# A graph attention layer's sums: from the planner's order to an order fixed in the source, with shares a chunk ahead and edge sums a chunk behind

## The chip, the cores and the metric

The kernel runs on one NeuronCore of a Trainium2 chip. Five engines run their own instruction queues side by side: TensorE (PE, matrix products; PEld is its loading of weights), VectorE (DVE), ScalarE (ACT), GpSimd (POOL) and SyncE (SP, which here only starts transfers). They wait for one another by semaphores, and each takes its own queue strictly in the order in which the program was laid down. The metric is the device time of one execution in microseconds (us); the median of the runs counts.

## The reference

Two graph layers over 6250 nodes with 128 features and 100000 edges, sorted by destination. The first is a pair of graph convolutions; this case is about the second, an attention layer, cut here to what matters:

```
z = h @ fc_w.T                      # 6250 x 128
rh = r_h @ fc_r_w.T                 # 100000 x 128, r_h are the edges' own features
e = leaky_relu(z[src] @ aw[0] + z[dst] @ aw[1] + rh @ aw[2])
ex = exp(e - segment_max(e, dst)[dst])
alpha = ex / segment_sum(ex, dst)[dst]
agg = segment_sum(alpha[:, None] * (z[src] + rh), dst)
out = relu(agg + z @ loop_w)        # then x = layernorm(x + out)
```

## The kernel before

The edges are cut into 49 chunks (`NC`) of 2048. Every chunk's destinations lie in a window of 144 nodes (`WC`), so what a chunk adds goes into 144 columns of a transposed sum (`acc2` for the node part, `sum_r` for the edge part). The program has four stages, one after the other: preparing and sorting the slots of the edges, the first convolution, the second convolution, and the attention. The second convolution runs under `tc.manual_schedule()`, that is, its instructions stay in the order of the source. In all other stages a planner at compile time places the instructions of each engine by its own priorities and costs, within the data's dependencies and the number of buffers; it may pull work far ahead of its place in the source. The change lies in the last stage (L979 to L1239), from about 1426 us of the span to the end.

**The work of one chunk** in that stage:

- `shares` (L1147): the weights of the softmax are brought into the slots' order. DVE makes two one-hot masks (`ohm` L1150, `ohg` L1152) and their product with the weights (`put` L1155); PE sums over them in 16 products (L1159); DVE reduces the result to `swt` (L1160).
- `pick` (L451): the rows z[src]. For 12 of the 17 slot groups of a chunk they are picked from the table `hot` in SBUF by 144 small products with one-hot masks (L460, three parts of four groups, each in a PSUM tile `g`); ACT copies them out with their weight (`got`, L465). The other five groups are gathered from DRAM by POOL (`far`, L469). DVE makes the one-hot window mask `wm` (L474).
- `weigh` (L478) multiplies the mask of the five gathered groups by `swt` on ACT; `scatter` (L484) sums a chunk's 17 groups into its window, 34 products on PE in one PSUM tile `win`. Both are done for the chunk before (`held`).
- `edge_part` (L1162): loads the edges' features in two halves (`et`, 512 KB each, L1171), makes the masks `ms` (L1176, L1178) and `pl` (L1180) on DVE, sums the edges in 32 products (`r`, L1189), has ACT copy the result (`sw`, L1194), and places it in the window with four products (L1200).
- `add_in` (L491) adds a window into `acc2` or `sum_r` on DVE (L493).
- `Pieces` and `out_of` (L412, L429) finish the output of four blocks of 128 nodes as soon as all their edges are in: load `fin`, products (`agg`, L421), addition and layer norm, store.

**The scores** for the softmax are a second stream of work, written as a generator `scores()` that stops at each `yield`. It goes batch by batch: `batches` has 2, 5 and then 7 chunks at a time. For each batch it does `ends` for the destinations (four chunks at a time; a load `dk`, a mask L1012, products L1017, a dozen small DVE instructions, a store `adg`), `starts` for the sources (each chunk in two halves: a load `rk` of 256 KB, DVE's mask L1038 and `ohb` L1040, 24 products L1045 into the tile `k`, DVE's `sel` L1048 and reduction `asr` L1049), and `softmax` over the rows of the batch (L1053: a load `ad`, five scans on DVE with products on PE between them, an exponential on ACT, a store `shd` and a load `al` in another layout). The scores of batch b+1 are dealt out beside the chunks of batch b, in the source at four places of each chunk (`beside`, `deal`). Since this stage is not under `manual_schedule`, that placing is the planner's first order only.

Of the kernel before, what the change touches and what calls it, by code (L numbers as in the profile page):

```python
# [9 lines left out]
F32 = mybir.dt.float32  # L10
# [9 lines left out]
P = 128  # L20
# [18 lines left out]
def gnn_kernel(ctx, tc, x, src, dst, ea, ew, W1, b1, W2, b2, fcw, fcrw, attn, loopw, out):  # L39
# [372 lines left out]
    def out_of(sum_x, sum_r, b0, n, xp, pool, tag):  # L412
# [6 lines left out]
        for b, nb in some:  # L419
            of = slice(b * P, b * P + nb)  # L420
            nc.tensor.matmul(agg[:nb, b - b0, :], sum_r[:, of], wfrT, start=True, stop=False)  # L421
            nc.tensor.matmul(agg[:nb, b - b0, :], sum_x[:, of], ident, start=False, stop=True)
        for p, k in whole(some, b0):
# [5 lines left out]
    class Pieces:  # L429
# [3 lines left out]
        def __init__(self, start):  # L433
            self.ahead = [(min((b0 + n) * P, N), start(b0, n)) for b0, n in groups]
            self.at = None
            next(self.ahead[0][1])

        def go(self, low, steps):

            while steps > 0:  # L440
                if self.at is None:
# [3 lines left out]
                    if self.ahead:  # L445
# [5 lines left out]
    def pick(c, mask, hot, table, ps_g, wp, gots=4, fars=12):  # L451

        rows = []
        for g0 in range(0, GP, 4):
# [11 lines left out]
            rows += [got[:, g, :] for g in range(n)]  # L466
        for g in range(GS):
# [5 lines left out]
        wm = wp.tile([P, G, WC], F32, name="wm")  # L473
        nc.vector.tensor_tensor(wm, iota[:, None, :WC].to_broadcast([P, G, WC]),  # L474
                                sdst[:, c, :, None].to_broadcast([P, G, WC]), op=OP.is_equal)
# [8 lines left out]
    def scatter(held, ps_w):  # L484
# [4 lines left out]
        return ps  # L489
# [490 lines left out]
    with tc.tile_pool(name="look", bufs=2) as lp, tc.tile_pool(name="conv3", bufs=2) as wp, \  # L980
            tc.tile_pool(name="mov", bufs=2) as mp, tc.tile_pool(name="outp", bufs=2) as xp, \
            tc.tile_pool(name="ps_g3", bufs=3, space=PSUM) as ps_g, tc.tile_pool(name="ps_w3", bufs=1, space=PSUM) as ps_w, \
            tc.tile_pool(name="ps_r3", bufs=1, space=PSUM) as ps_r, tc.tile_pool(name="ps_k3", bufs=1, space=PSUM) as ps_k, \
            tc.tile_pool(name="ps_c3", bufs=2, space=PSUM) as ps_c:
# [22 lines left out]
        def ends(c0, n):  # L1007
# [5 lines left out]
            ps = ps_c.tile([P, 4, J, NK], F32, name="rec")  # L1013
# [18 lines left out]
        def starts(c):  # L1032

            for h in range(2):
# [6 lines left out]
                                        op=OP.is_equal)  # L1041
                ps = ps_k.tile([P, NL // 2, NB], F32, name="k")
# [10 lines left out]
        def softmax(b):  # L1053
# [5 lines left out]
            ps = ps_c.tile([P, P], F32, name="rec")  # L1059
# [12 lines left out]
            def moved(k, of, way):  # L1072

                ps = ps_c.tile([P, 1], F32, name="rec")
# [6 lines left out]
            def spread(of, k):  # L1081

                nc.vector.tensor_tensor(of, of, end, op=OP.mult)
                nc.vector.tensor_tensor_scan(full[:, ::-1], go[:, ::-1], of[:, ::-1], 0.0, op0=OP.mult, op1=OP.add)
                ps = moved(k, full[:, 0:1], behind)
# [6 lines left out]
            nc.vector.tensor_tensor_scan(part, bias, e, -BIG, op0=OP.add, op1=OP.max)  # L1092
            ps = moved(0, part[:, P - 1 :], before)
# [8 lines left out]
            nc.vector.tensor_tensor_scan(part, first, e, 0.0, op0=OP.mult, op1=OP.add)  # L1102
# [306 lines left out]
```

## Time and profile before

| | us |
|---|---|
| median of 14 runs | 2312.17 (2294.31 to 2326.83) |
| the profiled execution | 2302.72 |
| its span | 2300.8 |
| granted clock of TensorE, mean | 0.865 |

How to read the lines below: in a timeline each line is a start, a duration, an engine, a line of the kernel, an operation, what it writes and reads, its shape, and how many in a row; in brackets stands how long the engine was idle before it, and what ended that. In a table of stretches each line has the stretch and its length, then for each engine the busy time and in brackets the count of instructions, then the granted clock of TensorE as a share, the share in which the DMA engines were busy and the GB/s that they moved. In a table of groups the busy time and the mean duration of one (in ns) follow the bar, then the idle time of the engine just before them and who ended it.

### The profile page before, as it was taken

What the parts mean: (1) busy time and instruction counts of PE and PEld (TensorE: products, weight loads), DVE (VectorE), ACT (ScalarE), POOL (GpSimd) and SP (SyncE); (2) the same over time, 40 slices, a digit from 0 to 9 for tenths busy, and PEclk for the clock granted to TensorE, in tenths of its full rate; (3) what the DMA queues carried; (4) which work ended last, traced back from release to release, by engine and by line L of the source; (5) the groups of instructions that cost most, each with busy time, mean ns of one, the idle gap of its engine ahead of it and who ended that gap; (6) DMA issues with size and microseconds to landing.
All of it is one profiled execution on the core that took longest, in us unless ns stands there. A gap on an engine that the chain in (4) does not pass through costs nothing.

```text
span 2300.8 us, 78659 instructions
## 1 busy us (share of the span) xinstructions
PE 1776.5 (77%) x33861; PEld 1546.2 (67%) x33861; DVE 1695.5 (74%) x3105; ACT 993.5 (43%) x3096; POOL 1185.3 (52%) x929
## 2 busy tenths in 40 slices
PE   3677788887988786788888883368887888888886
PEld 2465677776877665677777772367777777777775
DVE  8749786785867327788988874688787788787663
ACT  1106445444554554466666662023333333334443
POOL 4003655767766627768878760214243344436662
PEclk9758799998998877889999995579899898889998
DMA  3001433333343316576666765645555556555552
GB/s 82 2 1 57 131 88 114 86 94 91 82 122 111 110 54 216 154 210 225 223 205 219 227 187 94 148 128 159 152 148 148 141 145 167 143 148 144 153 158 66
DMA packets 260706, 306.79 MB, mean 133 GB/s; under 512 B 44121, under 2 KB 199372, under 8 KB 253299
## 3 DMA queue, kind: packets, MB, share of 16 engines
q1 hardware_dynamic: 228741, 244.80, 35.2%
q0 software_dynamic: 23520, 48.22, 10.2%
q10 hardware_dynamic: 8088, 8.65, 1.2%
q8 instruction: 268, 4.39, 0.8%
q14 instruction: 89, 0.73, 0.1%
HBM read 260.35 MB, written 41.23 MB: 131 GB/s over the span
## 4 chain that ended last, share of the span: by engine, by line
PE 44%; DVE 12%; issue 8%; DMA 6%; ACT 3%; another core or an unknown queue 2%; DVEq 0%; SPq 0%; POOL 0%; ACTq 0%
PE win L488 18%; PE g L460 13%; DVE wm L474 2%; PE rec L1159 2%; PE k L1045 2%; DVE sel L1048 2%; PE r L1189 2%; DMA et<-in_edge_attr_dram 2%; PE rec L1200 2%; PE mm L317 1%; DMA hz<-part 1%; ACT got L465 1%; DMA dk<-drow 1%; DVE asr L1049 1%
## 5 line engine op out<-in xcount | busy, mean ns | idle before, releaser
L469 POOL DMA_INDIRECT far<-g,sidx x490 | 766.2, 1564 | 312.2 <-PE win L488 183.2
L465 ACT ACTIVATE got<-g,swt 128x128 f32<-128x128 f32 x1764 | 489.6, 380 | 560.8 <-PE g L460 242.9
L460 PE MATMUL g<-hot,mask 128*32 128x128 bf16 x21168 | 503.3, 235 | 218.0 <-issue 200.9
L469 POOL DMA_INDIRECT far<-zd,sidx x245 | 345.7, 1411 | 531.4 <-PE win L488 402.9
L460 PEld LDWEIGHTS <-mask 128*32 128x32 bf16 x21168 | 379.2, 103 | 320.2 <-issue 300.3
L488 PE MATMUL win<-wm,got 128*128 128x144 f32 x3528 | 528.7, 308 | 5.5 <-issue 3.9
L488 PEld LDWEIGHTS win<-wm,got 128*128 128x128 f32 x3528 | 493.3, 207 | 26.3 <-issue 17.4
L474 DVE TENSOR_TENSOR wm<-iota,sdst 128x2448 f32<-128x2448 f32 x147 | 396.9, 2700 | 4.4 <-DMA g<-rows 4.4
L482 ACT ACTIVATE wm<-wm,swt 128x144 f32<-128x144 f32 x735 | 255.7, 427 | 76.4 <-DVE swt L1160 47.6
L488 PE MATMUL win<-wm,far 128*128 128x144 f32 x1470 | 208.0, 287 | 8.4 <-DMA far<-g,sidx 7.2
L488 PEld LDWEIGHTS win<-wm,far 128*128 128x128 f32 x1470 | 191.2, 190 | 10.2 <-issue 8.8
L1045 PE MATMUL k<-adp,rk 128*128 128x49 bf16 x2352 | 102.5, 198 | 79.2 <-DVE sel L1048 55.8
L1045 PEld LDWEIGHTS <-rk 128*128 128x128 bf16 x2352 | 90.5, 105 | 96.0 <-issue 53.1
L493 DVE TENSOR_TENSOR acc<-acc,win 128x144 f32 x147 | 44.1, 300 | 145.7 <-PE win L488 132.8
L306 POOL TENSOR_TENSOR hot<-low,hot 128x512 bf16<-128x512 f32 x24 | 42.2, 1758 | 200.0 <-DVE own L681 129.2
L931 DVE TENSOR_TENSOR et<-et,ar_row 128x2048 f32<-128x2048 f32 (+1 forms) x49 | 111.6, 2278 | 23.1 <-DMA et<-in_edge_attr_dram 21.5
L932 DVE TENSOR_REDUCE dots<-et 128x16 f32<-128x2048 f32 (+1 forms) x49 | 112.0, 2286 | 1.7
L1048 DVE TENSOR_TENSOR sel<-k,ohb 128x392 f32<-128x392 f32 x98 | 83.6, 853 | 29.3 <-PE k L1045 17.5
L730 PE MATMUL rec<-put,ohm 128*128 128x90 bf16 x784 | 62.1, 253 | 28.2 <-DVE put L726 26.6
L730 PEld LDWEIGHTS <-ohm 128*128 128x128 bf16 x784 | 57.1, 165 | 34.7 <-DVE put L726 29.0
L723 DVE TENSOR_TENSOR put<-ohg,rec 128x1360 bf16<-128x1360 bf16 x49 | 76.8, 1567 | 0.0
L676 ACT CAST own<-r 128x768 bf16<-128x768 f32 x49 | 39.6, 808 | 82.5 <-PE r L673 42.9
(380 smaller groups left out, 2312.8 us busy)
## 6 DMA issues: line engine op xcount, KB each, us to landing
et<-in_edge_attr_dram SPq DMA_DIRECT2D x97, 512.0 KB
et<-in_edge_attr_dram SPq DMA_DIRECT2D x48, 1024.0 KB
mask<-masks SPq DMA_DIRECT2D x98, 384.0 KB
rk<-srow SPq DMA_DIRECT2D x98, 256.0 KB
mask<-srd SPq DMA_DIRECT2D x49, 384.0 KB
masks<-mask SPq DMA_DIRECT2D x49, 384.0 KB
far<-g,sidx POOLq DMA_INDIRECT x490
g<-rows SPq DMA_DIRECT2D x24, 256.0 KB
```

The lines of the kernel that those rows point to most:

```text
L460: nc.tensor.matmul(ps[32 * q : 32 * q + 32, g, :], mask[:, (g0 + g) * P + 32 * q : (g0 + g) * P + 32 * q + 32], hot[:, 4 * (g0 + g) + q, k ...
L465: nc.scalar.activation(got[:, g, :], ps[:, g, :], AF.Copy, scale=swt[:, c, g0 + g : g0 + g + 1])
L469: nc.gpsimd.indirect_dma_start(out=got, out_offset=None, in_=table[:, :], in_offset=bass.IndirectOffsetOnAxis(ap=sidx[:, c, g : g + 1], ax ...
L474: nc.vector.tensor_tensor(wm, iota[:, None, :WC].to_broadcast([P, G, WC]), sdst[:, c, :, None].to_broadcast([P, G, WC]), op=OP.is_equal)
L482: nc.scalar.activation(wm[:, g, :], wm[:, g, :], AF.Copy, scale=swt[:, c, g : g + 1])
L488: nc.tensor.matmul(ps, rows[g], wm[:, g, :], start=g == 0, stop=g == G - 1)
L723: nc.vector.tensor_tensor(put[:, :, : G * F].rearrange("p t (g f) -> p t g f", f=F), ohg[:, :, :, None].to_broadcast([P, TC, G, F]), rec[: ...
L730: nc.tensor.matmul(ps, ohm[:, :, t], put[:, t, :], start=t == 0, stop=t == TC - 1)
L931: nc.vector.tensor_mul(et[:n], et[:n], ar_row[:n, None, :].to_broadcast([n, TC, D]))
L932: nc.vector.tensor_reduce(dots[:n, c, :], et[:n], AX.X, OP.add)
L1045: nc.tensor.matmul(ps[:, s, :], mk[:, s * P : (s + 1) * P], adp[:, 0, k, :NB], start=k == 0, stop=k == 2)
L1048: nc.vector.tensor_mul(sel, ps, ohb.rearrange("p b s -> p s b"))
```

## The change

The whole loop over the chunks is put under `tc.manual_schedule()`, so that every engine's order is that of the source; only the scores of batch 0 and the loads before the loop are still placed by the planner. To make that order, the pieces are cut finer:

- `pick` gets a callback `between`, which is called after each of its three parts. It deals a step of the scores, gives out a third of the window's products of the chunk before (`scattering`, 6, 6 and 5 groups), does a piece of other work, and deals another step. After part 0 the piece is placing the edge sums of the chunk before (`edge_places`) and making this chunk's edge masks; after part 1 it is adding those edge sums, a step of the output, and making the masks of the shares of the next chunk. `wm` comes first instead of last.
- After `pick` come the products of the next chunk's shares, a step, the edge sums (`edge_sums`), the reduction to `swt`, the addition into `acc2`, a step and a step of the output.
- So the shares run a chunk ahead, and the edge sums are placed and added a chunk behind. `lows` of the chunk before sets which blocks are ready for the output.
- `masks` are loaded a chunk ahead, `et` half a chunk to a chunk ahead.
- The scores get more places to stop (between what DVE makes and what PE takes, or after a load is issued), their own PSUM tile (`ps_s3`; `ps_g3` has two instead of three), and are dealt evenly over eight places of each chunk except the batch's last. `steps_of` counts the steps of a batch.
- `Pieces` no longer issues the load of the next group a group ahead, and `out_of` has one more stop.

The core of the diff (the stops added inside the softmax are all alike):

```diff
@@ out_of
             nc.tensor.matmul(agg[:nb, b - b0, :], sum_x[:, of], ident, start=False, stop=True)
+        yield
         for p, k in whole(some, b0):
...
-    def pick(c, mask, hot, table, ps_g, wp, gots=4, fars=12):
+    def node_masks(c, wp):
+        wm = wp.tile([P, G, WC], F32, name="wm")
+        nc.vector.tensor_tensor(wm, iota[:, None, :WC].to_broadcast([P, G, WC]),
+                                sdst[:, c, :, None].to_broadcast([P, G, WC]), op=OP.is_equal)
+        return wm
+
+    def pick(c, mask, hot, table, ps_g, wp, gots=4, fars=12, between=None):
+
 
         rows = []
+        if between:
+            wm = node_masks(c, wp)
         for g0 in range(0, GP, 4):
...
             rows += [got[:, g, :] for g in range(n)]
+            if between:
+                between(g0 // 4)
         for g in range(GS):
...
+    PARTS = -(-GP // 4)
+
+    def scattering(held, ps_w, count=PARTS):
+
         c, rows, wm = held
         ps = ps_w.tile([P, WC], F32, name="win")
         for g in range(G):
             nc.tensor.matmul(ps, rows[g], wm[:, g, :], start=g == 0, stop=g == G - 1)
-        return ps
+            if (g + 1) * count // G > g * count // G:
+                yield ps
...
-            tc.tile_pool(name="ps_g3", bufs=3, space=PSUM) as ps_g, tc.tile_pool(name="ps_w3", bufs=1, space=PSUM) as ps_w, \
+            tc.tile_pool(name="ps_g3", bufs=2, space=PSUM) as ps_g, tc.tile_pool(name="ps_w3", bufs=1, space=PSUM) as ps_w, \
             tc.tile_pool(name="ps_r3", bufs=1, space=PSUM) as ps_r, tc.tile_pool(name="ps_k3", bufs=1, space=PSUM) as ps_k, \
-            tc.tile_pool(name="ps_c3", bufs=2, space=PSUM) as ps_c:
+            tc.tile_pool(name="ps_s3", bufs=1, space=PSUM) as ps_s, tc.tile_pool(name="ps_c3", bufs=2, space=PSUM) as ps_c:
...
             nc.vector.tensor_scalar(dk[:, : n * P], dk[:, : n * P], iotap, None, op0=OP.is_equal)
-            ps = ps_c.tile([P, 4, J, NK], F32, name="rec")
+            yield
+            ps = ps_s.tile([P, 4, J, NK], F32, name="rec")
...
+        def steps_of(b):
+            n = min(batches[b][0] + batches[b][1], NC - 1) - batches[b][0] + (b == 0)
+            return 3 * -(-n // 4) + 4 * n + 16
...
+        POINTS = 2 * PARTS + 2
+        spots = []
         for b, (c0, n) in enumerate(batches):
+            more = steps_of(b + 1) if b + 1 < NT else 0
+            last_ = POINTS * max(n - 1, 1)
+            spots += [min(more, -(-more * (k + 1) // last_)) - min(more, -(-more * k // last_)) for k in range(POINTS * n)]
+        spots = iter(spots)
+
+        def deal():
+            for _ in range(next(spots)):
+                next(steps, None)
...
+        pieces = Pieces(lambda b0, n: out_of(acc2, sum_r, b0, n, xp, ps_c, "rec"), False)
+        while 0 not in ready:
+            next(steps)
+
+        with tc.manual_schedule():
+            load_masks(0)
+            load_edges(0)
+            al3, aw, i = batch_of(0)
+            nc.vector.tensor_reduce(swt[:, 0, :], shares(*share_masks(0, al3, i)), AX.X, OP.add)
+            held = edge = None
+            for c in range(NC):
+                load_masks(c + 1)
+                load_edges(2 * c + 1)
+                load_edges(2 * c + 2)
+                aw, i = batch_of(c)[1:]
+                low = lows[max(c - 1, 0)]
+                wins, now, adding = [], {}, None
                 if held is not None:
                     weigh(held)
-                    win = scatter(held, ps_w)
-                ps = edge_part(c, aw, c - c0)
-                beside()
+                    adding = scattering(held, ps_w)
+
+                def between(part):
+                    deal()
+                    if adding is not None:
+                        wins.append(next(adding))
+                    if part == 0:
+                        if edge is not None:
+                            now["sum"] = edge_places(*edge)
+                        now["edge"] = edge_masks(c, aw, i)
+                    elif part == 1:
+                        if edge is not None:
+                            add_in(sum_r, c - 1, now["sum"])
+                        pieces.go(low, 1)
+                        if c + 1 < NC:
+                            al3, _, k = batch_of(c + 1)
+                            now["share"] = share_masks(c + 1, al3, k)
+                    deal()
+
+                new = pick(c, masks_in.pop(c), hot, zd, ps_g, wp, 4, 11, between)
+                if c + 1 < NC:
+                    shared = shares(*now["share"])
+                deal()
+                ms, pl = now["edge"]
+                edge = *edge_sums(c, ms), pl
+                if c + 1 < NC:
+                    nc.vector.tensor_reduce(swt[:, c + 1, :], shared, AX.X, OP.add)
                 if held is not None:
-                    add_in(acc2, c - 1, win)
+                    add_in(acc2, c - 1, wins[-1])
                 held = new
-                add_in(sum_r, c, ps)
-                pieces.go(lows[c], 1)
-                beside()
-        weigh(held)
-        add_in(acc2, NC - 1, scatter(held, ps_w))
-        pieces.go(N, 999)
+                deal()
+                pieces.go(low, 1)
+            add_in(sum_r, NC - 1, edge_places(*edge))
+            weigh(held)
+            add_in(acc2, NC - 1, scatter(held, ps_w))
+            pieces.go(N, 999)
```

In the prediction, D1 to D8 are the eight places of a chunk at which `deal` is called, in order: D1 and D2 around the work after part 0 of `pick`, D3 and D4 after part 1, D5 and D6 after part 2, D7 after the shares, D8 at the chunk's end.

## The prediction

> **What bounds the kernel now.** First the page's busy shares:
>
> ```profile
> PE 1776.5 (77%) x33861; PEld 1546.2 (67%) x33861; DVE 1695.5 (74%) x3105; ACT 993.5 (43%) x3096; POOL 1185.3 (52%) x929
> ```
>
> No engine is full, so the stage is read alone. In the timeline each chunk ends with L493's addition into sum_r: chunk 1 at 1539.9 us, 6 at 1620.4, 34 at 2103.9, 41 at 2189.5, 48 at 2279.2. Busy time in stretches cut there (length, then PE, PEld, DVE, ACT, POOL; granted clock, DMA share):
>
> ```profile
> 1500.00:1540.00 40.00, 23.56 (x454) 21.33 (x452) 33.35 (x104) 5.78 (x22) 7.02 (x5) 0.64 0.46 122
> ...
> 1620.00:2104.00 484.00, 401.09 (x8220) 357.12 (x8219) 394.12 (x862) 175.32 (x559) 187.54 (x137) 0.88 0.55 148
> 2104.00:2190.00 86.00, 73.77 (x1611) 65.95 (x1610) 54.56 (x87) 40.38 (x135) 57.08 (x36) 0.98 0.60 159
> ```
>
> Up to chunk 34 a chunk takes 17.3 us (484/28), DVE 81% and PE 83% busy: neither is full, and each waits for the other. The last 14 hold no scores, because the planner pulled those ahead; they take 12.5 us on PE. The groups by form price DVE's work (busy, mean ns):
>
> ```profile
> L474 DVE TENSOR_TENSOR wm<-iota,sdst 128x2448 f32<-128x2448 f32 x58 | 156.5, 2698 | 0.0
> ...
> L1048 DVE TENSOR_TENSOR sel<-k,ohb 128x392 f32<-128x392 f32 x98 | 83.6, 853 | 29.3 <-PE k L1045 17.5 <-remote 4.3 <-PE rec L1200 3.9
> ...
> L1049 DVE TENSOR_REDUCE asr<-sel 128x8 f32<-128x392 f32 x98 | 54.3, 554 | 0.0
> L1038 DVE TENSOR_SCALAR rk<-rk,iotap 128x1024 bf16<-128x1024 bf16 x98 | 49.9, 509 | 18.6 <-DMA rk<-srow 18.6
> ```
>
> DVE's timeline shows two things: dense instructions follow 0.08 us earlier than their durations say (2.62 us after a wm of 2.70), and a load used soon after its issue is waited for.
>
> ```profile
> 1504.23 0.26 DVE L1012 TENSOR_SCALAR dk<-dk,iotap 128x128 bf16<-128x128 bf16 x1 [2.24 <-DMA dk<-drow]
> ...
> 1513.71 2.70 DVE L474 TENSOR_TENSOR wm<-iota,sdst 128x2448 f32<-128x2448 f32 x1
> 1516.33 0.56 DVE L1049 TENSOR_REDUCE asr<-sel 128x8 f32<-128x392 f32 x1
> ```
>
> A late chunk's timeline: a gather beside DVE's wm takes 3.24 us instead of 0.94, and PE waits for ACT's copy of the edge sums.
>
> ```profile
> 2212.92 0.94 POOL L469 DMA_INDIRECT far<-zd,sidx  x1 [2.10 <-PE win L488]
> ...
> 2213.89 2.70 DVE L474 TENSOR_TENSOR wm<-iota,sdst 128x2448 f32<-128x2448 f32 x1
> 2214.17 3.24 POOL L469 DMA_INDIRECT far<-zd,sidx  x1 [0.31 <-issue]
> ...
> 2215.62 0.76 PE L1200 MATMUL rec<-pl,sw 128*128 128x144 f32 x4 [0.38 <-ACT sw L1194]
> ```
>
> **The change, part by part.** *DVE's work stays.* Per chunk, spaced 0.08 less than recorded: wm 2.62, ms twice 0.60, pl 0.37, ohm 1.13, ohg 0.35, put 0.92, swt 0.13, two additions 0.44, 0.7 for output pieces and registers: 7.9. A half of a chunk's starts (sel, asr, rk, ohb) is 1.94. The scores of seven chunks are 14 halves (27), two ends of 2.3 and a softmax of 6.5: 38. So seven chunks ask 7 x 7.9 + 38 = 93 of DVE. Check: 28 chunks with the 64 halves of 1620 to 2104 ask 398; the row has 394.
>
> *PE in a chunk without scores.* Dense runs in the chain and the timeline give g 2.23 for 144, win 4.36 for 34, shares 1.14, r 0.81, places 0.54, k 0.78 for 24 (a half of a chunk). With about 1.2 of g's issue gaps and 0.5 of pieces: 10.8. What goes is the wait for ACT's copy (0.5 and 0.38 in the late chunk), because edge_places uses the sums of the chunk before. More is unhidden: PE waits for nothing of its own chunk but the masks for shares, and DVE finishes those at 7.9 us, when PE has done 8.2. I take 10.8 (ends: 10.0, the row's busy time per late chunk, and 12.5, today's).
>
> *Waits that the fixed order adds.* There are eight deals in a chunk, one step in each; a step on DVE and one on PE alternate and need each other. Between D4, D5 and D6 DVE has nothing else in its queue, so it waits there until PE's 24 matmuls are through (0.78 and the handing over, less ohb beside them: 0.7). Behind the waiting sel sit all of DVE's later steps, swt's reduction and the next wm; behind PE's blocked k sit win's third part, shares, r and the next chunk's g. In the chunks with four halves (7.9 + 7.8 = 15.7) DVE then waits 0.7 between D4 and D6, 0.7 for shares and 0.45 before D8, or 0.7 alone when the parity turns: 17.5, 17.5 and 16.4. PE comes near too: its 10.8 becomes 12 at the clock of 0.88, with four halves 16; I add 1.0 to each for both being late in turn. In the others: dk, issued one step before its use and behind 1 MB of et on SP, 3.6 with the reply of its matmuls (the row above shows 2.24 of it, the chain lists dk loads of 3.3 to 4.5); Exp behind its table load of 1.28, 1.8; al, whose store and load take 5.4 from e (L1111 at 1488.5) to its use (L233 at 1493.9), two deals on, 3.3; in the last chunk, which has no deals, PE exceeds DVE by 2.9. Sum per seven chunks: 93 + 1.9 + 1.9 + 0.7 + 3 + 3.6 + 1.8 + 3.3 + 2.9 = 112. Chunks 7 to 41 are five such: 560, before 569 (2189.5 - 1620.4): -9. Bounds: no wait of DVE, 5 x 96 = 480; every wait doubled, 640. I stay at the walked order, as stage two, in an order fixed by hand as well, also left DVE 16% idle (326.46 of 390 us busy).
>
> *The other queues.* SP now takes mask(c+1), et(2c+1) and et(2c+2) at a chunk's head, where they wait for r of the chunk before; they are used at the next chunk's g and at this chunk's r, over 10 us later, so their landing is hidden. rk, fin, out, adgd, ad, shd and al stand behind them. rk is asked for two halves (some 8 us) ahead of its use and lands in 3.1 to 3.5 by the chain: hidden, and if et holds it up by 1 MB at 148 GB/s, 7 us, the excess of 2 or 3 would fall on DVE in one chunk of three, 30 in all; I count none of it. POOL issues far behind the third part of g, a whole chunk ahead of its use, with eleven buffers for ten rows: hidden. ACT's 12 got, 5 weighings and one copy are 3.2 + 1.6 + 0.4 in its dense runs, half of a chunk; sw is copied at once and used a chunk later.
>
> *Chunks 2 to 6.* 50 steps on 32 points, so half the points have two, and the second depends on the first: 77 of work, 22 of such waits, 3 for the free last chunk: 102. Before 80.5, since the planner had done 23 of 98 halves by 1540. +22 (bounds 0 and +45).
>
> *Start.* Softmax of batch 0 no longer shares DVE: shares(0) come 5 earlier, at 1494. But batch 1's 42 steps, which the planner ran from 1470 beside the load of hot, now lie in the eight deals of chunk 0: ten halves of 2.6 with PE's reply, two ends with an exposed dk 12, softmax with its round trips 19, chunk 0's own 7 less 4 of overlap: 60. With chunk 1 (10.8) chunk 2 begins at 1565, before about 1538: +27 (bounds +10, where waits overlap, and +40).
>
> *Last seven chunks.* 7 x 10.8 = 76, before 89.7: -14 (bounds -20 and 0).
>
> *End.* The group of blocks 44 to 46 is released a chunk later, so its products now lie behind the last scatter (4.4) and addition rather than ahead of them, and then the single fin buffer still makes its store, the next load and the last group follow (2284.3 to 2292.9): +6. The finer early loads, masks a chunk ahead, one PSUM bank moved from g to the scores: free, since ACT takes a part in 1.1 us and PE comes back to the bank after 5; were that cover gone, one 1.1 per chunk, 50.
>
> Sum: 27 + 22 - 9 - 14 + 6 = +32 on the profiled 2302.7, that is 2335; the median of the runs is 9.5 higher. I round to **2340**.
>
> **Weighed against the skill.** Row: gathers have a mean of 1.41 and 0.30 between, 8.6 per chunk; one beside wm is 3.24. I keep 8.6 to 9.9, under every period. The Trainium skill, SBUF — State Buffer, "SBUF: two separate sides", says that DVE's two-port instructions lock GpSimd out for their whole length, so that a denser DVE starves gathers. If all five were held as long as beside wm, that would be 17.7 per chunk and 2440. The clock row is 0.88 with PE 83% busy. The Trainium skill, TensorE: Matmul & The Clock Gate, Part 1, says that about 3.4 us of idleness is what throttles PE; my added waits are shorter, so by it PE stays fast, the 15 us for both being late go, and the sum is 2325.
>
> **Rivals.** *The order packs well* (faster): feasible, because wm, masks and sm stand between most deals. Without the extra lateness and with half the other waits, chunks 7 to 41 take 512 and 2 to 6 take 91: 27 + 10 - 57 - 14 + 6 = -28, 2285. It decides where DVE's waits in chunks 2 to 41 fall under 1.8 us per chunk, at which the gain there pays for the start; my sum has 2.6. Against it: 0.81 of DVE in the planner's order, which could reorder round each wait. *PE late at every reply*: 16 us of PE at 0.88 beside 15.7 of DVE; at 20 per full chunk, 17 chunks x 2 more: 2375. For: the clock row; against: other chunks let PE catch up. *POOL becomes the bound* from five held gathers: 17.7 x 14 late chunks is 97 more, 2435. For: 3.24 beside wm; against: POOL sat waiting for win 402.9 us, so it has slack. *Nothing moves*: prologue loss equals the gain at the end, 2312.
>
> **How the numbers follow.** Two runs differ by about 0.3% with no change. Forecast (2312 to 2365) 0.44, of which 0.07 within 0.3%; packing 0.34, of which 0.03 within; PE late 0.15; POOL 0.07. Faster 0.31, same 0.10, slower 0.59. The range runs from packing with nearly no wait (2255) to PE late with a long start (2405).
>
> **What would show it.** In the new trace: chunk 2 begins near 1565; the last seven chunks near 10.8 without scores before them; in chunks with four halves DVE waits for k (L1045's line) once or twice, 0.7 each; DVE waits for dk and al once per batch; L1200 no longer waits for ACT; the end 29 after the last r. Wrong if DVE is over 90% busy from chunk 7 to 41 (packing), if PE's rows exceed DVE's there, or if far's mean passes 2 us.

## The result, and the profile after

| | before | after |
|---|---|---|
| median of the runs beside each other, us | 2308.61 (47 runs) | 2478.71 (10 runs, 2441.96 to 2495.49) |
| ratio | | 1.0673, interval 1.0629 to 1.0717 |
| span of the profiled execution | 2300.8 | 2475.6 |
| granted clock, mean | 0.865 | 0.844 |

The changed kernel is slower by 6.7%, where 1.2% was forecast (2340, up to 2405). The ratios and their intervals, here and below, leave out the executions that took over 1.5% longer than the fastest of their kernel (one of E10, of 4920 us, among them), while medians are of all, so that the two medians above divide to 1.074. The page has the same instructions on PE (33861) and DVE (3105), with more busy time on both and smaller shares:

```profile
PE 1818.9 (73%) x33861; PEld 1568.5 (63%) x33861; DVE 1752.9 (71%) x3105; ACT 991.6 (40%) x3096; POOL 1136.7 (46%) x929
```

From here on chunks are cut at the end of the edge sums' last product (L1189 before, L1227 after; the forecast cut at L493's addition, up to 7 us later). In the table of stretches of the kernel after, the rows are chunks 7 to 34, 35 to 41 and the last seven (length, then PE, PEld, DVE, ACT, POOL, clock, DMA):

```profile
1684.00:2247.00 563.00, 407.31 (x8098) 356.49 (x8096) 407.52 (x830) 172.71 (x556) 149.64 (x139) 0.87 0.49 127
2247.00:2358.00 111.00, 89.48 (x1874) 78.61 (x1870) 85.98 (x157) 42.98 (x140) 41.98 (x36) 0.94 0.51 139
2358.00:2450.00 92.00, 81.64 (x1628) 71.64 (x1622) 55.94 (x89) 40.30 (x139) 40.60 (x32) 0.93 0.51 131
```

A chunk takes 20.1 us (563/28) with PE and DVE each 72% busy: neither engine bounds, and both stand idle more than before (83% and 81%). The next table gives the lengths by stage; the forecast's column is its own marks plus its terms (1620.4 + 49, 560, 89.7 - 14, 21.6 + 6):

| us | forecast | before | after | before, second kind of chip | after, second kind |
|---|---|---|---|---|---|
| end of chunk 6 | 1669 | 1613.5 | 1683.6 | 1486.5 | 1542.1 |
| chunks 7 to 41 | 560 | 574.2 | 674.5 | 497.5 | 603.0 |
| last seven | 76 | 90.3 | 91.4 | 78.7 | 71.2 |
| from there to the end | 27.6 | 22.8 | 26.1 | 22.9 | 26.1 |

The last two columns need a sentence: the runs E5 to E16 went to chips on which the kernel before takes 2091 to 2094 us instead of 2304 (E1 to E4) to 2309 (the table above), so they are compared among themselves, and E9 and E13 are the two kernels there. By the spans the loss is 175 us on the first kind of chip and 157 on the second. The larger part lies in chunks 7 to 41 (100 and 105 us), most of the rest ahead of them (70 and 56).

The groups by form leave DVE's durations where they were (856 ns for sel, 853 before), and show who is waited for now. A gather takes 1.12 us instead of 1.41:

```profile
L1069 DVE TENSOR_TENSOR sel<-k,ohb 128x392 f32<-128x392 f32 x98 | 83.9, 856 | 82.0 <-remote 49.3 <-PE k L1066 22.8 <-PE rec L1188 9.8
...
L1058 DVE TENSOR_SCALAR rk<-rk,iotap 128x1024 bf16<-128x1024 bf16 x98 | 50.9, 519 | 24.5 <-DMA rk<-srow 24.5
```

```profile
L482 POOL DMA_INDIRECT far<-zd,sidx x245 | 274.7, 1121 | 746.9 <-PE win L503 640.4 <-issue 102.3 <-PE r L1227 3.6
```

The waits of after in chunks 7 to 41 (total in us, times, longest), DVE and then PE; "remote" means that the profile finds nobody who released it then:

```profile
DVE sel L1069 <- remote: 44.4, 11, 4.3
DVE pl L1212 <- PE rec L1242: 31.3, 17, 3.2
DVE swt L1316 <- PE rec L1188: 24.9, 21, 2.7
DVE dk L1031 <- DMA dk<-drow: 19.1, 6, 4.1
DVE al L233 <- DMA al<-shd: 12.3, 5, 6.0
```

```profile
PE k L1066 <- DVE rk L1058: 68.5, 41, 4.3
PE r L1227 <- issue: 31.7, 58, 1.0
PE g L471 <- issue: 24.3, 43, 1.2
```

Two places of the timeline show how the first two rows of DVE come about. First, for pl: PE's products k stand in its queue before a mask that DVE has not made, and behind them stand the window's products and the placing of the edge sums (L1242). DVE's pl has one buffer, which those placing products still hold, so after its own wait PE makes DVE wait (and the window's products take 3.21 us here, 1.74 elsewhere: more on this at the clock, below):

```profile
1967.50 0.79 PE L1066 MATMUL k<-adp,rk 128*128 128x49 bf16 x24 [2.53 <-DVE rk L1058]
1968.13 3.21 PE L503 MATMUL win<-wm,got 128*128 128x144 f32 x12
1971.14 0.87 PE L1242 MATMUL rec<-pl,sw 128*128 128x144 f32 x4
```

```profile
1972.05 0.46 DVE L1212 TENSOR_TENSOR pl<-iota,place 128x288 f32<-128x288 f32 x1 [3.00 <-PE rec L1242]
```

Second, for sel: PE's products trickle, a handful per 0.7 us, without a wait that the profile shows. The 24 products k were through at 1982.8 by their modelled end; DVE's sel, which needs them, starts at 1987.68, when the trickle of r is nearly over:

```profile
1982.69 0.43 PE L1227 MATMUL r<-et,ms 128*32 128x128 f32 x8
...
1984.75 0.44 PE L1227 MATMUL r<-et,ms 128*32 128x128 f32 x5 [0.31 <-issue]
1986.20 0.43 PE L1227 MATMUL r<-et,ms 128*32 128x128 f32 x4 [1.00 <-issue]
...
1987.63 0.33 PE L1227 MATMUL r<-et,ms 128*32 128x128 f32 x3 [0.45 <-issue]
```

```profile
1987.68 0.95 DVE L1069 TENSOR_TENSOR sel<-k,ohb 128x392 f32<-128x392 f32 x1 [4.29 <-remote]
```

### The profile page after: what moved, and what is told of

The parts are those of the page before. It is cut to its first block, busy times and chain, and to the rows that moved or that the text cites. A ratio compares the mean times of both kernels' runs of the same rounds, so it can differ in the third digit from the quotient of the medians.

```text
span 2475.6 us, 78565 instructions
## 1 busy us (share of the span) xinstructions
PE 1818.9 (73%) x33861; PEld 1568.5 (63%) x33861; DVE 1752.9 (71%) x3105; ACT 991.6 (40%) x3096; POOL 1136.7 (46%) x929
## 4 chain that ended last, share of the span: by engine, by line
PE 49%; DVE 28%; issue 11%; DMA 5%; another core or an unknown queue 3%; ACT 2%; SPq 1%; POOL 1%; DVEq 1%; ACTq 0%; POOLq 0%
PE win L503 20%; PE g L471 13%; DVE wm L455 4%; DVE sel L1069 2%; PE rec L1188 2%; PE k L1066 2%; PE r L1227 1%; DVE ohm L1176 1%; PE r L692 1%; DVE rk L1058 1%; DVE asr L1070 1%; DVE put L742 1%; DVE put L1181 1%; PE rec L749 1%
## 5 line engine op out<-in xcount | busy, mean ns | idle before, releaser
L482 POOL DMA_INDIRECT far<-g,sidx x490 | 788.3, 1609 | 312.4 <-PE win L503 183.6
L482 POOL DMA_INDIRECT far<-zd,sidx x245 | 274.7, 1121 | 746.9 <-PE win L503 640.4
L503 PE MATMUL win<-wm,got 128*128 128x144 f32 x3528 | 543.2, 313 | 1.4 <-issue 0.8
L503 PEld LDWEIGHTS win<-wm,got 128*128 128x128 f32 x3528 | 503.2, 210 | 22.5 <-issue 12.5
L503 PE MATMUL win<-wm,far 128*128 128x144 f32 x1470 | 219.5, 298 | 11.5 <-DMA far<-g,sidx 11.5
L1066 PE MATMUL k<-adp,rk 128*128 128x49 bf16 x2352 | 91.0, 196 | 141.0 <-DVE rk L1058 101.2
L1066 PEld LDWEIGHTS <-rk 128*128 128x128 bf16 x2352 | 80.7, 104 | 156.4 <-DVE rk L1058 138.4
L1233 ACT COPY sw<-r 128x256 f32<-128x256 f32 (+1 forms) x49 | 18.1, 370 | 333.6 <-PE r L1227 202.3
L512 DVE TENSOR_TENSOR acc<-acc,win 128x144 f32 x147 | 44.4, 302 | 119.2 <-PE win L503 77.9
L951 DVE TENSOR_REDUCE dots<-et 128x16 f32<-128x2048 f32 (+1 forms) x49 | 112.0, 2286 | 1.7
L1227 PE MATMUL r<-et,ms 128*32 128x128 f32 x1564 | 84.1, 305 | 34.6 <-issue 33.7
L1227 PEld LDWEIGHTS r<-et,ms 128*32 128x32 f32 x1564 | 50.6, 120 | 53.4 <-issue 50.1
L749 PE MATMUL rec<-put,ohm 128*128 128x90 bf16 x784 | 62.4, 254 | 27.6 <-DVE put L745 26.0
```

What stands on the lines that cost most here:

```text
L482: nc.gpsimd.indirect_dma_start(out=got, out_offset=None, in_=table[:, :], in_offset=bass.IndirectOffsetOnAxis(ap=sidx[:, c, g : g + 1], ax ...
L503: nc.tensor.matmul(ps, rows[g], wm[:, g, :], start=g == 0, stop=g == G - 1)
L749: nc.tensor.matmul(ps, ohm[:, :, t], put[:, t, :], start=t == 0, stop=t == TC - 1)
L951: nc.vector.tensor_reduce(dots[:n, c, :], et[:n], AX.X, OP.add)
L1066: nc.tensor.matmul(ps[:, s, :], mk[:, s * P : (s + 1) * P], adp[:, 0, k, :NB], start=k == 0, stop=k == 2)
L1227: nc.tensor.matmul(ps[WS * q : WS * q + WS, g, :], ms[:p, s, :], edges_in[2 * c + g][:p, s % 8, :], start=half == 0, stop=half == 1 or s + ...
```

## Experiments

Theories at the outset: the loss is that of the *fixed order* (an engine stands before what isn't ready, and cannot take the next thing), against *the restructuring itself* (shares ahead, edge sums behind, finer steps). Then: which waits, and which of them are on the path.

### E1: the changed source in the planner's order

```diff
-        with tc.manual_schedule():
+        if True:
```

> The changed source without the fixed order: the loop over the chunks is left to the planner again, and everything else of the change stays (parts, shares a chunk ahead, edge sums a chunk behind, two PSUM banks for g, more stops). Theory (the fixed order is what costs: each engine's head waits for another engine while work that is ready stands behind it): back to about the kernel before, 2280 to 2330. Rival (the restructuring costs, not the order: fewer banks, smaller pieces, work later): it stays near the changed kernel, 2420 or more.

Measured: 2231.61, ratio to before 0.9708 (0.9601 to 0.9815). Some 247 us lie between the two orders of the same source, and the planner makes the restructured source the fastest kernel on this kind of chip. Chunks 7 to 41 and the last seven:

```profile
1597.00:2125.00 528.00, 453.16 (x9958) 400.38 (x9947) 461.58 (x1008) 219.22 (x696) 246.52 (x176) 0.96 0.60 165
2125.00:2201.00 76.00, 73.64 (x1626) 66.16 (x1623) 51.81 (x88) 41.02 (x136) 51.84 (x33) 1.00 0.62 159
```

DVE is busy 462 us for the same work that takes it 494 in the fixed order (407.52 + 85.98): the first sign that not only waits had grown.

### E2, E3, E4: three places singly

E2 moves the window's products ahead of the step in `between`; E3 gives pl two buffers (and sw one, for room); E4 computes batch 1's scores before the loop.

```diff
@@ E2
-                    deal()
                     if adding is not None:
                         wins.append(next(adding))
+                    deal()
@@ E3
-            pl = mp.tile([P, NL // 8, WC], F32, name="pl", bufs=1)
+            pl = mp.tile([P, NL // 8, WC], F32, name="pl", bufs=2)
-            sw = mp.tile([P, NL // 8, D], F32, name="sw")
+            sw = mp.tile([P, NL // 8, D], F32, name="sw", bufs=1)
@@ E4
-            more = steps_of(b + 1) if b + 1 < NT else 0
+            more = steps_of(b + 1) if 0 < b < NT - 1 else 0
-        while 0 not in ready:
+        while 1 not in ready:
```

> In the fixed order, a part of the window's products is put ahead of the deal after each part of pick, not behind it. Theory (PE's step of the scores, k, stands at its queue's head and waits for DVE's rk, 69 of 675 us in chunks 7 to 41, while ready window products stand behind it): PE then has 1.5 us of work for each such wait, its waits for rk halve, and since edge_places also comes earlier, DVE's wait for pl goes; 40 to 60 less, near 2425. Rival (DVE's own chain sets the pace, PE's waits there are slack): within 10 of the changed kernel, 2470 to 2490.

> In the fixed order, the mask pl gets two buffers (and sw one, for the room). Theory (DVE's writing of pl waits for PE's edge_places, the reader of the old pl, 45 us in all, with all of DVE's later work behind it): 25 to 45 less, 2435 to 2455, and the wait of pl is gone from the waits. Rival (DVE only comes earlier to its next wait, sel for k): less than 10, 2470 or more.

> The scores of batch 1 are done before the loop, by the planner, as those of batch 0 are, instead of 42 steps in the eight deals of chunk 0. Theory (those steps run there one behind the other, while the planner did them beside the load of the table and the softmax of batch 0): the end of chunk 1's r, 1573 us now, comes 25 to 45 earlier, and the whole is 2435 to 2455. Rival (the work is only moved, DVE is as busy before the loop): within 8 of the changed kernel.

| | us | ratio to before (after: 1.0673) |
|---|---|---|
| E2 | 2432.42 | 1.0583 (1.0490 to 1.0676) |
| E3 | 2452.15 | 1.0659 (1.0564 to 1.0753) |
| E4 | 2462.28 | 1.0735 (1.0621 to 1.0849) |

By the medians 46, 27 and 16 us less than after; by the ratios, whose intervals overlap that of after, only E2 stands out. From 1500 to 2450 us sel's wait for "remote" falls from 44.4 to 18.1 us in E2, where r hardly trickles any more (its "issue" 6.1 instead of 33.7), while PE waits for rk as before (111.7 and 101.2). In E3 the wait of pl (44.9) is gone, and sum_r waits for the same placing products instead (20.0). In E4 chunk 1 ends 37 us earlier (1536.5 against 1573.1), and chunk 48 only 11 (2438.3 against 2449.5). E2's time came near what was expected of it (2425), but not for the reason given, since the wait for rk was to halve. No single place holds the loss.

### E5 to E8: other places, on the second kind of chip

E5 puts r ahead of the shares' products. E6 makes the scores' masks of the next half beside this half's products. E7 is E2 to E6 together; E8 is E5 and E6 in the planner's order.

```diff
@@ E5
-                if c + 1 < NC:
-                    shared = shares(*now["share"])
-                deal()
                 ms, pl = now["edge"]
                 edge = *edge_sums(c, ms), pl
+                if c + 1 < NC:
+                    shared = shares(*now["share"])
+                deal()
@@ E6, starts(c0, c1); masks_of(i) makes rk and ohb of half i
+            made = masks_of(2 * c0)
+            yield
+            for i in range(2 * c0, 2 * c1 + 2):
+                mk, ohb = made
...
+                if i < 2 * c1 + 1:
+                    made = masks_of(i + 1)
                 yield
                 sel = lp.tile([P, NL // 2, NB], F32, name="sel", bufs=1)
```

> The edge sums' 32 products (r) are put ahead of the shares' 16, nothing else. In the changed kernel PE's instructions trickle after r (three gaps of 0.45 us in most of the last seven chunks), the word that k or r is done then comes 2 to 5 us late: DVE's sel waits 44 us in chunks 7 to 41 and ACT's sw 34 us in the last seven. Theory: it is the unbroken row of small products r, then g, that runs PE's supply dry; with the shares between them the trickle shortens, sel's late waits fall under 20 us, the last seven chunks take about 84 instead of 91, and the time falls to 2410 to 2440. Rival: the trickle comes wherever PE is in step with its supply, so it only moves to the shares and delays swt instead: 2460 to 2490.

> Of the scores' starts, DVE's masks for the next half (rk and ohb) are made in the step in which PE gets this half's 24 products, so that PE's k finds its mask made two deals earlier. Theory: PE's k standing before a mask that is not made yet is what the forecast missed. PE's wait for rk, 101 us from 1500 to 2450, falls under 25; with it DVE's wait of pl for the placing products behind k (45) under 20; the time falls by 60 to 110, to 2370 to 2420. Rival: DVE sets the pace and PE's wait was only its slack, so the wait goes to another line (shares or sel) and the time stays within 20 of 2479.

> Fixed order with five edits together: batch 1's scores before the loop, the window's products ahead of the step, two buffers for pl (and one for sw), r ahead of the shares, and the starts' masks a half ahead. Three of them alone gave 16, 46 and 27. Theory: each wait is a place of its own, so the gains add up to most of the 170 lost, 2300 to 2350, with chunks 7 to 41 at 16 to 16.8 each, near the walked order. Rival: they share the same waits, so that the sum is hardly more than the best of them, 2380 to 2430.

> The changed source in the planner's order (that alone gave 2232), with r ahead of the shares and the starts' masks a half ahead. If the order on paper matters only where it is fixed, the planner makes of both sources the same, 2220 to 2245. If the masks made ahead take a wait away for the planner too (its PE waits 30 us for sel and rk from 1450 on), 2195 to 2220.

The numbers of these expectations were for the first kind of chip; the changed kernel itself takes 2244.46 here (E9). "Gaps" are counted from the trace: all of PE's idle times of 0.3 to 1.3 us, whoever ended them.

| | us | against E9 or E10 | ratio to before |
|---|---|---|---|
| E5 | 2280.97 | +36.5 | 1.0903 (1.0855 to 1.0950) |
| E6 | 2226.38 | -18.1 | 1.0640 (1.0592 to 1.0687) |
| E7 | 2217.16 | -27.3 | 1.0608 (1.0564 to 1.0653) |
| E8 | 2075.74 | -6.3 (E10) | 0.9900 (0.9839 to 0.9961) |

E5: the theory of the unbroken row of small products could not show itself, since PE's gaps are 13 us in chunks 7 to 48 of the changed kernel here (E9) and not 78 as on the first kind (and those before which the profile names nobody 0 and not 65); what the edit costs shows in DVE's wait for the shares behind r, 19.6 us in E9 and 53.3 here. E6: PE's wait of 75.6 for rk falls to 12.0 as the theory said, and comes back as a wait for the one PSUM buffer of k, which sel holds:

```profile
PE k L1071 <- DVE sel L1076: 46.9, 32, 4.2
PE rec L1037 <- DVE dk L1031: 38.9, 8, 9.2
PE k L1071 <- DVE rk L1058: 12.0, 5, 5.4
```

So the rival was right here: most of PE's wait was slack, and DVE set the pace. E7 (E5's loss among its five edits) gains little more than E6 alone. E8 is not told apart from E10.

### E9, E10, E11, E12: controls, a load and the spacing on DVE

E9 and E10 repeat the changed kernel and E1. E11 issues dk when the products of the group before are issued:

```diff
@@ E11, ends(); targets(i) issues the load of group i
-            dk = lp.tile([P, 4 * P], BF16, name="dk", bufs=1)
-            nc.sync.dma_start(dk[:, : n * P], drow[c0 : c0 + n, :].rearrange("(o c) p -> o (c p)", o=1).to_broadcast([P, n * P]))
+            i, dk = dks.pop(c0)
             yield
...
+            targets(i + 1)
```

E12 only changes the order of DVE's instructions: the second of a pair no longer stands right behind the first that it needs.

```diff
@@ E12: sel, rk of the next half, asr; ms, ohg, ms; ohm, put
                 nc.vector.tensor_mul(sel, ps, ohb.rearrange("p b s -> p s b"))
-                nc.vector.tensor_reduce(asr[:, 1 + c * NL + of.start : 1 + c * NL + of.stop], sel, AX.X, OP.add)
+                if i < 2 * c1 + 1:
+                    mk = mask_of(i + 1)
+                nc.vector.tensor_reduce(asr[:, 1 + i * NL // 2 : 1 + (i + 1) * NL // 2], sel, AX.X, OP.add)
...
+            ohg = hot_ and groups_hot(c + 1)
             nc.vector.tensor_mul(ms, ms, aw[:, i, :, None].to_broadcast([P, NL, WS]))
```

> The changed kernel as it is, beside the kernel before on this chip, as the measure for the other three and for the four of the call before, whose chip ran the kernel before in 2091 us rather than 2304. There PE stood for want of instructions 19 to 20 us in chunks 7 to 48 (here 78). Theory: the loss comes from the order that is fixed, not from that, so the ratio to the kernel before is again 1.06 to 1.09 on any chip. Rival: want of instructions and the late semaphores behind it are the loss; then a chip without them shows 0.98 to 1.03.

> The changed source in the planner's order, again, on the same chip as the three others. Theory: 0.96 to 0.99 of the kernel before, DVE's time from start to start 468 for chunks 7 to 41 as in the first run of it (the fixed order has 519). Rival, that its gain was that chip's: 1.0 or more.

> Fixed order; the load dk is issued as soon as the products of the group before are through, instead of one step before its use. In the changed kernel DVE waits 19 us for it in chunks 7 to 41 and PE 18 to 35 for DVE's mask behind it. Theory: these waits stand on the path, since everything behind them is queued: 20 to 40 us less than the changed kernel on the same chip. Rival: they are taken up by other waits: within 10.

> Fixed order; on DVE alone three pairs of which the second needs the first at once are set apart: the next half's rk goes between sel and asr, ohg between the two ms, ohm between ohg and put. No instruction more or less. From start to start sel takes 0.89 us in the changed kernel and 0.79 in the planner's order, ms 0.71 and 0.62, ohg 0.47 and 0.37. Theory: a result that is used at once costs 0.1 us of spacing that my sum left out; sel, ms and ohg fall back to these, DVE's time from start to start in chunks 7 to 41 falls by 15 to 20, and the time by 10 to 25. Rival: the spacing is due to waits on semaphores, not to the dependence: sel, ms and ohg stay, and the time is within 8.

| | us | ratio to before |
|---|---|---|
| E9 | 2244.46 | 1.0749 (1.0703 to 1.0795) |
| E10 | 2082.05 | 0.9972 (0.9941 to 1.0003) |
| E11 | 2211.66 | 1.0592 (1.0519 to 1.0666) |
| E12 | 2211.26 | 1.0571 (1.0499 to 1.0642) |

E9: against the kernel before, the fixed order loses as much where PE does not run short of instructions, so the loss does not need that. Here it costs 162 us against E10 where it cost 247 against E1, so on the first kind the shortage may add some of these 85; this was not tested apart. The restructuring by itself gains nothing here that can be told: E10 is 0.3% below the kernel before. E1's 3% belong to the first kind of chip. The stretch of chunks 7 to 41 and DVE's waits in E9:

```profile
1542.00:2145.00 603.00, 457.02 (x9974) 419.01 (x9974) 491.56 (x987) 216.22 (x696) 205.88 (x174) 0.89 0.55 145
```

```profile
DVE dk L1031 <- DMA dk<-drow: 20.2, 7, 4.1
DVE swt L1316 <- PE rec L1188: 19.6, 13, 4.8
DVE pl L1212 <- PE rec L1242: 17.7, 11, 3.7
DVE al L233 <- DMA al<-shd: 14.3, 5, 5.7
DVE sel L1069 <- PE k L1066: 11.4, 17, 1.0
```

E12 shows the other half. In E9's timeline asr starts 0.87 us after sel, which it needs, though sel lasts 0.83:

```profile
1700.50 0.83 DVE L1069 TENSOR_TENSOR sel<-k,ohb 128x392 f32<-128x392 f32 x1
1701.37 0.56 DVE L1070 TENSOR_REDUCE asr<-sel 128x8 f32<-128x392 f32 x1
1701.85 0.48 DVE L1058 TENSOR_SCALAR rk<-rk,iotap 128x1024 bf16<-128x1024 bf16 x1
```

In E10 the planner has put something between, and in E12 the source has: the next start comes 0.76 and 0.75 after sel's.

```profile
1700.14 0.85 DVE L1069 TENSOR_TENSOR sel<-k,ohb 128x392 f32<-128x392 f32 x1
1700.90 0.68 DVE L1208 TENSOR_TENSOR ms<-iota,rels 128x512 f32<-128x512 f32 x1
1701.51 0.55 DVE L1070 TENSOR_REDUCE asr<-sel 128x8 f32<-128x392 f32 x1
```

```profile
1703.37 0.83 DVE L1073 TENSOR_TENSOR sel<-k,ohb 128x392 f32<-128x392 f32 x1
1704.12 0.48 DVE L1057 TENSOR_SCALAR rk<-rk,iotap 128x1024 bf16<-128x1024 bf16 x1
1704.52 0.55 DVE L1076 TENSOR_REDUCE asr<-sel 128x8 f32<-128x392 f32 x1
```

Over chunks 7 to 41 DVE's work from start to start (to the next instruction's start, or the own duration and 0.1 us where that comes later) is 514 us in E9, 463 in E10 and 497 in E12, a wm (2.6 us) more or less by where the stretch is cut; sel falls from 0.90 to 0.79, ms from 0.69 to 0.63, ohg from 0.47 to 0.35. Counted over the same chunks, E9 has 345 neighbours on DVE of which the second reads what the first has just written; by the median it starts 0.035 us after the recorded end of the first. The other neighbours without a longer wait (539) start 0.083 before it. E10 has 39 such pairs and E12 212, so 306 pairs at 0.118 make 36 of the 51 us between E9 and E10, and 133 pairs make 16 of the 17 between E9 and E12. The theory of the spacing is right. The time falls by 33, and spacing is not all of that: the swap also puts rk ahead of asr, so that PE finds its mask earlier (its wait for rk falls from 75.6 to 57.9 us, that of sel for k from 11.4 to 5.5). What each is worth in time was not separated. E11 is as good: the wait for dk is gone, PE's behind it falls from 38.1 to 20.9.

### E13 to E16: the kernel before on this chip, and sums of edits

E14 is E11 and E12 together; E15 adds the edits of E2 and E4; E16 is E14 in the planner's order.

> The kernel before as it is, for its trace on this chip. On a chip of the second kind (2092 us) theory: PE's gaps for want of instructions, 71 us in chunks 7 to 48 on the first chip, are under 30, and the stage from chunk 7 to 41 takes 480 to 520 instead of 574, so that the loss of the fixed order there is 80 to 120 of 603. Rival: the gaps stay and the difference lies in the three stages before.

> Fixed order with dk loaded ahead and the three pairs set apart, which alone gave 33 us each. If they are terms of a sum, 55 to 70 less than the changed kernel on the same chip (2244 there, so 2175 to 2190; on a chip of the first kind 2410 to 2425). If both free the same time, 30 to 45.

> Those two, and batch 1's scores before the loop, and the window's products ahead of the step. Batch 1 alone gave 16 and brought the end of chunk 1 forward by 36; the window's products gave 46 on a chip where PE ran short of instructions. Theory: here the window's products are worth under 15, batch 1's scores 10 to 25: 2140 to 2170. Rival: batch 1's scores only move work in front of the loop: no better than 2175.

> The changed source with dk loaded ahead and the pairs set apart, in the planner's order. The planner sets the pairs apart by itself (sel 0.79 from start to start) and waits only 6 us for dk, so theory: within 10 of the planner's order of the changed source (2082 there). Rival: 15 or more better, which would mean that the source held these faults in any order.

E13: 2087.54 (one run; its expectation holds). PE's gaps are 29 us in chunks 7 to 48, and chunks 7 to 41 take 497.5:

```profile
1487.00:1984.00 497.00, 428.27 (x9821) 395.47 (x9819) 446.10 (x951) 214.95 (x693) 249.35 (x176) 0.95 0.64 173
```

| | us | against E9 or E10 | ratio to before |
|---|---|---|---|
| E14 | 2171.29 | -73.2 | 1.0400 (1.0330 to 1.0469) |
| E15 | 2160.42 | -84.0 | 1.0324 (1.0273 to 1.0375) |
| E16 | 2081.70 | -0.4 (E10) | 0.9941 (0.9906 to 0.9976) |

The load and the pairs are terms of a sum (33 + 33, together 73), and nearly half of the 162 that the fixing costs here. The two other edits add 11, of which 6 by the end of chunk 6. In the planner's order neither is worth anything that can be told: it had done both by itself (E10 waits 5.7 us for dk). No fixed order that was tried reaches the kernel before; of the planner's, E1 beats both kernels on the first kind of chip and E8 and E16 by 0.6 to 1% on the second.

## Why the prediction was wrong

The sign was right, the size not: 139 us short. By the spans it is 143 (2475.6 against 2300.8 + 32): 114 in chunks 7 to 41, 14 before them, 16 in the last seven. Chunks 7 to 41 are laid out per seven chunks of scores, as the forecast did (93 of DVE's work and 19 of waits):

| per seven chunks, us | length | DVE from start to start | rest |
|---|---|---|---|
| forecast | 112 | 93 | 19 |
| before, first kind; second (E13) | 114.8; 99.5 | 92.5; 91.0 | 22.3; 8.5 |
| after, first kind | 134.9 | 103.8 | 31.1 |
| after, second kind (E9) | 120.6 | 102.8 | 17.8 |
| planner's order (E1; E10) | 105.7; 99.7 | 93.6; 92.5 | 12.2; 7.1 |
| E14 | 110.6 | 99.4 | 11.1 |

Set against the row of the kernel before, DVE's work from start to start makes some 57 of the 100 us that chunks 7 to 41 lose on the first kind of chip, and some 60 of the 105 on the second; the rest is waits.

**"DVE's work stays"** is the step that failed on both kinds of chip. The 0.08 us less than recorded, read from an instruction beside another that did not need it, is no property of the instruction but of its neighbour: the planner strings unrelated instructions together, the source's order puts a result's use right behind it. It costs 10.8 us per seven chunks, 54 of the 114, and E12 takes a third of it away by order alone. The check in the forecast (398 against 394) was made on the planner's order and could not see it. The profile before did hold it, in the second convolution, whose order was fixed already: dots (L932) reads what L931 has just written and starts 0.03 us after its end, in all 49 chunks, while L931 here starts 0.08 before the end of the wm ahead of it:

```profile
1178.36 2.70 DVE L474 TENSOR_TENSOR wm<-iota,sdst 128x2448 f32<-128x2448 f32 x1
1180.98 2.29 DVE L931 TENSOR_TENSOR et<-et,ar_row 128x2048 f32<-128x2048 f32 x1
1183.30 2.29 DVE L932 TENSOR_REDUCE dots<-et 128x16 f32<-128x2048 f32 x1
```

**"Waits that the fixed order adds"** had the right sum where PE is fed: 17.8 against 19. Term by term dk was given 3.6 per batch and took 4.0 (20.2 in five), al 3.3 and took 2.9, k 0.7 a time and took 0.67 (11.4 in 17); the wait of pl for the placing products, 3.5 per batch, was not seen, as PE's wait for the mask of k was taken to touch nobody. Shares were given 1.4 per batch and took 3.9 (19.6 in five), Exp 1.8 and took 0.2 (0.8 in five), and the 3 for both engines being late and the 2.9 for the last chunk have no rows of their own. So that the sum came out is in part luck. On the first kind of chip the waits are the second step that failed, with 31.1 for 19, the other 60 of the 114: the difference to the second kind is 13.3 x 5 = 66, of which sel's 44.4 behind the trickle is the larger part, and the 13.6 that pl waits more the next. PE's trickle was known from g in the profile before (31.7 us there). That DVE can be held up with nobody named, the profile before showed only in small (sel's "remote" 4.3 in the forecast's own line, and swt 7.0 in chunks 7 to 41); that it would grow to 44 with r trickling, no row showed.

**"PE in a chunk without scores", 10.8,** is right on the second kind (10.2; E10 has 10.0) and in the planner's order on the first (10.85), and wrong there in the fixed order (13.1): in five of the last seven chunks PE trickled at the head of g, 8.8 us in all, of the 15.5 by which they are longer than in E1; DVE's waits for PE grew there too (from 21 to 32 us). The gain of 14 shrank to 7.5 and to a loss of 1.

**Start and chunks 2 to 6** were +49 and became +70 and +56. Of the 70, 7 were there before the changed stage (the last reduction of L932, L951 in the kernel after, ends at 1393.6 and 1400.5). E4 shows the mechanism right: batch 1's scores in chunk 0 cost 37 at the end of chunk 1. **End:** +6 forecast, +3 on both.

**The rivals.** DVE was 73% busy, so the order did not pack. "PE late at every reply" came nearest by its time, 19.3 us per chunk (674.5/35) where it had 20 in 17 of them, and E6 shows that PE's lateness was not what it cost on the second kind; that the time came near is luck. POOL fell away: far's mean stayed under 2 us (and its 97 counted 14 late chunks, of which the new order has seven). As forecast, L1242 no longer waits for ACT (0.2 us in the stage; L1200 before: 28.6 in chunks 7 to 41).

**The rule of the clock.** The mean wait of PE for rk was 1.7 us (68.5 in 41). That is under the 3.4 us or so of idleness at which, by the Trainium skill's page TensorE: Matmul & The Clock Gate, Part 1, PE is throttled, and by which the sum would have been 2325. The trace disagrees: after the gap of 2.53 us shown above the granted clock is 0.53, and 12 products take 3.21 us instead of 1.74. Of the 16 gaps of 2 to 3 us after 1500 us, 12 are followed by a mean clock under 0.75 in the next 3 us.

```profile
1964.00:1968.00 4.00, 1.25 (x58) 1.08 (x59) 3.97 (x6) 2.92 (x10) 3.45 (x2) 1.00 0.71 202
1968.00:1971.00 3.00, 3.00 (x24) 3.00 (x20) 1.01 (x2) 0.00 (x0) 0.00 (x0) 0.53 1.11 322
```

The clock is also a rival cause that no run separates. Over chunks 7 to 41 it has a mean of 0.89 in E9, 0.92 in E14 and 0.96 in E10; on the first kind of chip of 0.88 after, 0.90 before and 0.96 in E1. It is low where PE waits, and products at half speed make DVE wait longer: of the 3.00 before pl above, about 1.5 is the longer time of the 12 products (3.21 for 1.74). So part of the waits in the table may be the clock's.

**Open:** how much of the waits is the clock's; why PE runs short of instructions on one kind of chip and not on the other, and why the fixed order does so in the last seven chunks where E1, with the same instructions, hardly does.

## What to carry to other kernels

An order fixed in the source is priced by pairs, not by instructions: count for each engine how often an instruction needs the one right ahead of it (0.1 us each on DVE here), and set something between. The stage of a planner's order gives the durations of instructions but not the spacing that another order will have; a stage whose order is fixed already, in the same profile, can give it. Where PE was fed and DVE set the pace, a load earlier for DVE (33) and its pairs apart (33) paid most; freeing PE of its longest wait paid 18 (E6), where most of that wait came back as one for sel.

## What the runs showed of the hardware

- DVE starts an independent instruction about 0.08 us before the recorded end of the one ahead, and one that needs its result 0.035 after it (medians of 539 and 345 pairs in E9; 0.083 and 0.034 in E10). The Trainium skill's page VectorE: DVE Perf Modes, section "The DRAIN you can't avoid", says of a row of copies that a semaphore behind each costs nothing. No run here has such copies; where the next instruction needs the result, the pair costs 0.1 us more here.
- When PE trickles, DVE can start late on a product that is through by its modelled end: 4.9 us after the last of 24 products in the example (4.3 of them idle), 44 us of sel's idle time in chunks 7 to 41, and not once on the second kind of chip. That the word of the completion is what comes late is a reading of this; the profile names nobody.
- Chips differ by 10% on one program: 2304 to 2309 against 2091 to 2094, with some 71 and 29 us of PE's gaps in chunks 7 to 48, of which 46 and 1 have no releaser in the profile. A ratio found on one kind (0.971 for E1) was 0.997 on the other.
